# Pooling the key and value maps after their projection instead of pooling their input

## The chip, the cores and the metric

The program runs on one core of a Trainium2 chip. Its metric is the device time of one execution in microseconds (us); lower is better. A core has five engines that run side by side, each with its own queue in order: TensorE (PE, matrix products), VectorE (DVE), ScalarE (ACT, activations), GpSimd (POOL) and SyncE (SP, which issues DMAs). They wait for one another through semaphores. All data is fp32.

## The reference, cut to what matters

The input is 8 images of 256 channels at 32x32. Two layers follow; the change is in the first, a convolutional attention:

```python
q = einsum('bchw,oc->bohw', x, q_w)               # x is group-normalised
kv = einsum('bchw,oc->bohw', x, kv_w)
k_map, v_map = kv[:, :C], kv[:, C:]
def pooled(t):
    for i, r in enumerate([1, 2, 3, 6]):          # 32x32, 16x16, 11x11, 5x5
        p = einsum('bchw,ph,qw->bcpq', t, Mh, Mw) # mean over windows
        p = p + depthwise3x3(p, dconv_w[i], dconv_b[i])
    return concat of all p                        # 1024 + 256 + 121 + 25 = 1426 tokens
k = layernorm(pooled(k_map)); v = layernorm(pooled(v_map))
attn = softmax(q_g @ k^T * SCALE); out = attn @ v # 8 heads of 32 channels
```

Pooling works on positions and the projection on channels, so the two can be exchanged: a map projected from pooled x equals the pooled projection of x. After some mixing by head and a projection, layer 1 does self-attention over the 1024 tokens of each image, and a mixture of 8 experts (three dense steps each) over all tokens.

## The kernel before, in words

Channels lie on partitions, in two blocks of 128. An image of x is `xi`, [128, 2, 1024]. Keys and values are four maps of 128 channels and 1426 columns: m = 2 and 3 are values, 0 and 1 keys.

**Order of work.** The class `Flow` writes the program out ahead of time. It keeps an estimated clock for every engine, prices each instruction (`cost`) and emits them in one order per engine (`note`). Pieces of work are generators ("threads") with a rank. Before each piece they say what they wait for: `pe(...)`, `ve(...)`, `act(...)`, `pool(...)` or a condition (`until`). `step` runs those that are ready by the estimate and that fit: PE work fits when it ends before the score tile comes free, and within a credit of PE time per step (4.0 us for ranks under 5, 2.0 us for ranks from 5 on, which are layer 1). `finish` runs threads until a condition holds, ready or not. Every instruction of a flow has the line of the helper (669) in the profile, so the tile names tell the rows apart.

**The backbone** is a loop of 384 steps: 8 images x 2 channel blocks x 2 halves of the queries x 12 chunks of 128 keys (the last has 18). A step is the scores of one chunk for four heads (`sc`, one PSUM tile of four banks, one buffer), the exponential on ACT into `pt`, and the products with the values (`pv`) of the step before. Every second step POOL issues a DMA that adds one `pt` to the other (`pt<-pt`), and DVE adds such pairs up for the softmax sum. An image is 48 steps. The steps of image b + 1 can't begin before its keys are there: the loop calls `finish` on `key_parts`.

**Threads beside it**, by rank: keys and values to tokens (2; `keys_and_values`, `value_tokens`, `key_tokens`), preparation of the next image (4; `prepare`, with `pool_levels`, `maps`, `queries`), layer 1 and the set-up of its weights (5, 6), and the depthwise convolution (7; `convolve`).

- `prepare(b)` loads and normalises `xi`. `pool_levels(xi, xl)` makes the three pooled levels of x in `xl`, [128, 2, 402]: 16x16 and 11x11 on POOL (ten operations per block), 5x5 on DVE (5 reductions along rows, 5 along columns, one scaling).
- `maps` projects the four maps. Each has slices of 512, 512 and 402 columns (`KEY_SLICES`), the last from `xl`. A slice is two products of 128x128 weights with the slice, in PSUM (`sm` or `sx`). ACT copies it to `p` (`pmap`, one buffer) and, with bias and the middle tap (plus 1 for the identity), into the sum `acc` (three buffers).
- `taps` adds the other eight taps of a level on DVE, in place: acc = p * w + acc. `convolve` runs the four levels of one map after the other. `read` counts maps whose full-size level is convolved (then `p` may be overwritten there), `done` those that are finished, `freed` buffers given back.
- `queries` projects q from `xi` and stores it in DRAM.
- For image 0 `first_maps`, `first_keys` and `first_taps` do the same with more help from PE.

While the score loop runs, products with 128 weight columns are issued as four of 32 columns (`f.columns`, `narrow`). [...]one product of a 512- or 402-column slice with one of the two channel blocks leaves 8 records in the trace.

After the last step the remaining layer-1 work and the experts follow; expert passes run ahead of the gate while layer 1 ends, their results parked in DRAM. The program also holds a general version of everything, for inputs whose softmax sums go out of range; it is compiled, and skipped at the end by a branch.

Of the kernel before, what the change touches and what calls it, by code (L numbers as in the profile page):

```python
# [16 lines left out]
P = 128  # L17
# [638 lines left out]
class Flow:  # L656
# [162 lines left out]
    def keys(self, a):  # L819

        name = self.key(a)
        cut = self.cut.get(name)
        if cut is None:
            return [name]
        return [f"{name}/{i}" for i in range(len(cut) - 1) if cut[i] < a.offset + a.free_size() and a.offset < cut[i + 1]]
# [69 lines left out]
def attention(tc, kit, f, outer, ended, nb, consts, x, t1, t2, hn, bounds, vecs, q_t, kv_t, proj_t, gqk_t, wqk, wqkv, vecs1, w1_d, w1c, gate_d, wrc, vecs2, bnvec):  # L895
# [6 lines left out]
    with ExitStack() as ctx:  # L902
# [57 lines left out]
        )  # L960
        hi, lo = bounds
# [105 lines left out]
        todo, done, read, freed, key_parts, normalised = [], [], [4], [0], [0], [0]  # L1067
# [20 lines left out]
        def maps(xp):  # L1088

            for m in (2, 3, 0, 1):  # L1090
                c = m % 2
                yield until(lambda: read[0] >= len(todo) and len(todo) < 3 + 2 * freed[0])
                p = pmap
                acc = T(work, [P, NK], "acc", bufs=3)
                for s0, w in KEY_SLICES:
                    if s0 >= HW:
                        yield until(lambda: len(done) >= len(todo))
                    src = source(xp, s0, w)
                    yield pe(src, tag="sm")
                    ps = small()  # L1100
                    for k in range(2):
                        f.pe.matmul(
                            ps[:, :w],
                            lhsT=kvw[:, k, m * P : (m + 1) * P],
                            rhs=src[:, k, :],
                            start=k == 0,
                            stop=k == 1,
                        )
                    f.act.activation(p[:, s0 : s0 + w], ps[:, :w], AF.Copy)
                    for s, n in enumerate(SIDES):  # L1110
                        a, z = max(OFFS[s], s0), min(OFFS[s] + n * n, s0 + w)
                        if a < z:
                            f.act.activation(
                                acc[:, a:z],
                                ps[:, a - s0 : z - s0],
                                AF.Identity,
                                bias=db(c, s),
                                scale=mid[:, c * 4 + s : c * 4 + s + 1],
                            )
                todo.append((c, p, acc))  # L1120
# [7 lines left out]
        pmap = T(work, [P, NK], "p")  # L1128
        f.split(pmap, 512, HW)
# [14 lines left out]
        def first_maps(xp):  # L1144


            for m in range(4):
                if m < 2:
                    p = T(work, [P, 4, 512], "pt", bufs=6).rearrange("p j q -> p (j q)")
                    acc = T(l1, [P, NK], "v") if m else T(work, [P, NK], "kn", bufs=3)  # L1150
                else:
                    p = T(work, [P, NK], "acc", bufs=3) if m == 3 else pmap
                    acc = T(work, [P, NK], "acc", bufs=3)
                for t in (p, acc):
                    if t is not pmap:
                        f.split(t, 512, HW)
                first[m] = p, acc
            for m, s0 in [(m, s0) for g in (0, 2) for s0 in (0, 512) for m in (g, g + 1)] + [(m, HW) for m in range(4)]:
                if s0 == HW:
                    yield until(lambda: pooled)  # L1160
                w = min(512, NK - s0)
                c = m % 2
                p, acc = first[m]
                src = source(xp, s0, w)
                yield pe(src, tag="sm")
                ps = small()
                for k in range(2):
                    f.pe.matmul(
                        ps[:, :w],
                        lhsT=kvw[:, k, m * P : (m + 1) * P],  # L1170
                        rhs=src[:, k, :],
                        start=k == 0,
                        stop=k == 1,
                    )
                f.act.activation(p[:, s0 : s0 + w], ps[:, :w], AF.Copy)
                for s, n in enumerate(SIDES):
                    a, z = max(OFFS[s], s0), min(OFFS[s] + n * n, s0 + w)
                    if a < z and (m >= 2 or s):
                        f.act.activation(
                            acc[:, a:z],  # L1180
                            ps[:, a - s0 : z - s0],
                            AF.Identity,
                            bias=db(c, s),
                            scale=mid[:, c * 4 + s : c * 4 + s + 1],
                        )
                if (m, s0) == (3, 512):
                    large.append("maps")
                    f.spawn(first_keys(0), 1)
                    f.spawn(first_keys(1), 5)
            whole.append("maps")  # L1190
# [24 lines left out]
        def taps(c, s, p, acc):  # L1215
            n, o = SIDES[s], OFFS[s]
            pin = p[:, o : o + n * n].rearrange("p (h w) -> p h w", h=n)
            pout = acc[:, o : o + n * n].rearrange("p (h w) -> p h w", h=n)
            for tap in range(9):
                if tap == 4:  # L1220
                    continue
                dy, dx, y0, y1, x0, x1 = windows(tap, n)
                o_ap = pout[:, y0:y1, x0:x1]
                yield ve(pin[:, y0 + dy : y1 + dy, x0 + dx : x1 + dx], o_ap)
                f.ve.scalar_tensor_tensor(
                    o_ap, pin[:, y0 + dy : y1 + dy, x0 + dx : x1 + dx], dw(c, s, tap), o_ap, ALU.mult, ALU.add
                )

        def first_taps():
            for m in (2, 3):  # L1230
                yield until(lambda: "maps" in large)
                yield from taps(m - 2, 0, *first[m])
                large.append(("values", m))
            yield until(lambda: whole)
# [4 lines left out]
            done.extend(first[m][1] for m in (2, 3, 0, 1))  # L1239

        def convolve():

            for m in range(4, 4 * nb):
                yield until(lambda: len(todo) > m)
                c, p, acc = todo[m]
                for s in range(4):
                    yield from taps(c, s, p, acc)
                    read[0] += s == 0
# [51 lines left out]
        def pool_levels(xi, xl):  # L1300
# [6 lines left out]

            for k in range(2):
                one, l2, l3 = img[:, k], level(1)[:, k], level(2)[:, k]

                yield pool(xi)
# [3 lines left out]
                f.pool.tensor_tensor(l2, t2[:, 0::2, :], t2[:, 1::2, :], ALU.add)  # L1315
                yield pool(t2)
                f.pool.tensor_scalar(l2, l2, 0.25, 1.0, ALU.mult, ALU.mult)

                yield pool(xi)
                t3 = T(work, [P, 32, 11], "pool")  # L1320
                f.pool.tensor_tensor(t3, one[:, :, 0::3], one[:, :, 1::3], ALU.add)
                yield pool(t3)
                f.pool.tensor_tensor(t3[:, :, 0:10], t3[:, :, 0:10], one[:, :, 2::3], ALU.add)
                yield pool(t3)
                f.pool.tensor_tensor(t3[:, :, 1:11], t3[:, :, 1:11], one[:, :, 2::3], ALU.add)
                yield pool(t3)
                f.pool.tensor_tensor(l3, t3[:, 0::3, :], t3[:, 1::3, :], ALU.add)
                f.pool.tensor_tensor(l3[:, 0:10, :], l3[:, 0:10, :], t3[:, 2::3, :], ALU.add)
                yield pool(t3)
                f.pool.tensor_tensor(l3[:, 1:11, :], l3[:, 1:11, :], t3[:, 2::3, :], ALU.add)  # L1330
                flat = xl[:, k, OFFS[2] - HW : OFFS[3] - HW]
                f.pool.tensor_tensor(flat, flat, con[:, K_S11 : K_S11 + 121], ALU.mult)

            t5 = T(work, [P, 2, 32, 5], "pool")
# [4 lines left out]
            yield ve(t5, xl)  # L1339
            l5 = level(3)  # L1340
            for i, (a, e) in enumerate(ends):
                f.ve.tensor_reduce(
                    l5[:, :, i, :], t5[:, :, a:e, :].rearrange("p k h w -> p k w h"), AX.X, ALU.add
                )
            flat = xl[:, :, OFFS[3] - HW :]
            f.ve.tensor_tensor(flat, flat, con[:, None, K_S5 : K_S5 + 25].to_broadcast([P, 2, 25]), ALU.mult)
            pooled.append(True)

        def prepare(b):
# [35 lines left out]
            xl = T(work, [P, 2, NK - HW], "xl")  # L1385
            if b == 0:
                f.spawn(pool_levels(xi, xl), 2)
            else:
                yield from pool_levels(xi, xl)
            xp = xi, xl  # L1390
            if b == 0:
                todo.extend([None] * 4)
                f.spawn(queries(b, xi), 3)
                yield from first_maps(xp)
            else:
                yield from maps(xp)
# [64 lines left out]
        def keys_and_values(b):  # L1461
# [10 lines left out]
            if b == 0:  # L1472
                yield until(lambda: len(vts[b]) == 3)
                freed[0] += 1
# [1075 lines left out]
```

## Time and profile before

| | before |
|---|---|
| runs, us | 3309.33, 3313.4, 3316.51; median 3313.4 |
| profiled execution, us | 3310.0 (span 3308.1) |
| mean granted TensorE clock | 0.979 |
| matmul records | 23038 |

The span is the time from the first to the last instruction of the profiled execution; 1.9 us lie around it. Busy time of an engine is the time in which at least one of its instructions runs. PE instructions overlap, so a group's busy time is smaller than count times mean, and the distance of two starts is the better price of a group. A wait is put down to the instruction that released it.

### The profile page before, as it was taken

Reading aid. Unit: us, or ns where it says so; the run is one execution under the profiler, and the core shown is the slowest. Engines: PE = TensorE matmul, PEld = TensorE weight load, DVE = VectorE, ACT = ScalarE, POOL = GpSimd, SP = SyncE. Lnnn points to the kernel's source line nnn. Section 1 sums busy time; section 2 is a strip of 40 time slices with the busy share of each in tenths; the row PEclk is TensorE's granted clock in tenths of the full one; section 3 lists DMA queues with packets and bytes.
Section 4 is the critical chain, followed back from the end, with each engine's and each line's share of the span. In section 5 each row is a group of like instructions: output and inputs, shape, how many; then the busy total and the mean of one; then the engine's idle time right before and its main releaser. Section 6 shows DMA issues by size and latency. Waiting matters only on the chain. (4 is left out here: it accounts for less than half of the span.)

```text
span 3308.1 us, 57168 instructions
## 1 busy us (share of the span) xinstructions
PE 3098.8 (94%) x23038; PEld 1790.7 (54%) x23038; DVE 2455.2 (74%) x4068; ACT 1733.4 (52%) x2330; POOL 1217.1 (37%) x1315
## 2 busy tenths in 40 slices
PE   8687899999999999999899889999999999999997
PEld 4322234334334334334334236767888888888886
DVE  5687688797886887987875455447888787777776
ACT  4476675675676576666666543343333344444442
POOL 2211411412213213213112112007656567777775
PEclk9798999999999999999999999999999999999999
DMA  2357655745646756655556557125434310000000
GB/s 75 84 127 165 131 100 145 147 93 143 142 103 143 147 132 131 132 133 114 125 127 143 122 119 246 60 86 178 153 134 153 139 65 20 20 25 27 20 14 21
DMA packets 110754, 362.70 MB, mean 110 GB/s; under 512 B 13504, under 2 KB 38856, under 8 KB 87248
## 3 DMA queue, kind: packets, MB, share of 16 engines
q0 software_dynamic: 28608, 179.85, 28.2%
q1 hardware_dynamic: 78512, 177.13, 15.5%
q8 instruction: 184, 3.01, 0.4%
q10 hardware_dynamic: 3360, 1.97, 0.2%
q14 instruction: 90, 0.74, 0.1%
HBM read 112.45 MB, written 81.31 MB: 59 GB/s over the span
## 5 line engine op out<-in xcount | busy, mean ns | idle before, releaser
L669 ACT ACTIVATE pt<-sc 128x2048 f32<-128x2048 f32 (+1 forms) x384 | 720.5, 1876 | 298.5 <-PE sc L669 246.5
L669 DVE SCALAR_TENSOR_TENSOR acc<-p,vec,acc 128x225 f32<-128x225 f32 (+7 forms) x928 | 532.7, 580 | 31.3 <-ACT acc L669 6.5
L669 PE MATMUL sc<-q,kn 32*128 32x512 f32 (+1 forms) x3072 | 448.1, 653 | 108.0 <-ACT pt L669 105.8
L669 DVE TENSOR_TENSOR pt<-pt,pt 128x1024 f32<-128x1024 f32 x320 | 384.4, 1244 | 144.3 <-DMA pt<-pt 133.1
L669 POOL DMA_DIRECT2D pt<-pt x192 | 171.4, 894 | 769.3 <-ACT pt L669 592.9
L669 PE MATMUL pv<-pt,vt 128*32 128x512 f32 (+1 forms) x3072 | 420.2, 620 | 0.0
L669 ACT ACTIVATE p1c<-bank 128x256 f32<-128x256 f32 x230 | 87.9, 382 | 565.9 <-PE bank L669 554.3
L669 ACT ACTIVATE h<-h,bnvec 128x512 f32<-128x512 f32 x460 | 348.0, 805 | 63.8 <-DVE h L669 54.7
L669 POOL TENSOR_TENSOR rstd<-rstd,mhalf 128x4 f32<-128x4 f32 (+2 forms) x88 | 108.8, 1237 | 697.7 <-DVE rstd L669 586.3
L669 DVE TENSOR_TENSOR h<-p1c,bank 128x512 f32<-128x512 f32 x230 | 156.7, 681 | 211.6 <-PE bank L669 211.0
L669 PEld LDWEIGHTS sc<-q,kn 32*128 32x128 f32 (+1 forms) x3072 | 116.8, 179 | 320.2 <-ACT pt L669 217.8
L669 POOL TENSOR_TENSOR tm<-h,tm 128x256 f32<-128x256 f32 x210 | 241.8, 1151 | 16.5
L669 DVE TENSOR_TENSOR h<-u,bank 128x256 f32<-128x256 f32 x460 | 234.3, 550 | 7.9
L669 PEld LDWEIGHTS pv<-pt,vt 128*32 128x32 f32 (+1 forms) x3072 | 60.9, 108 | 304.2 <-issue 295.1
L669 POOL TENSOR_TENSOR tm<-h 128x512 f32<-128x512 f32 x105 | 137.9, 1313 | 195.2 <-ACT h L669 194.1
L669 DVE TENSOR_TENSOR h<-h,gate 128x1024 f32<-128x1024 f32 x128 | 203.2, 1588 | 0.5 <-ACT h L669 0.5
L669 PE MATMUL bank<-h,w2e 128*128 128x256 f32 (+1 forms) x604 | 193.3, 448 | 2.8 <-DVE h L669 1.9
L669 PE MATMUL sm<-p,v 128*32 128x256 f32 (+1 forms) x2416 | 192.3, 379 | 0.7 <-ACT p L669 0.7
L669 PE MATMUL y<-t,s3e 128*128 128x256 f32 x768 | 187.0, 379 | 2.2 <-POOL t L669 2.1
L669 PE MATMUL bank<-t,s1e 128*128 128x256 f32 x750 | 183.8, 381 | 3.5 <-DVE h L669 3.5
L669 POOL TENSOR_TENSOR t<-h,t 128x256 f32<-128x256 f32 x216 | 172.9, 800 | 17.0
L669 POOL TENSOR_TENSOR t<-h 128x512 f32<-128x512 f32 x108 | 140.1, 1298 | 105.4 <-DVE h L669 80.0
(315 smaller groups left out, 5448.6 us busy)
## 6 DMA issues: line engine op xcount, KB each, us to landing
pt<-pt POOLq DMA_DIRECT2D x160, 1024.0 KB, 7.5
h<-h SPq DMA_DIRECT2D x118, 512.0 KB, 3.3
xi<-in_x_dram SPq DMA_DIRECT2D x16, 512.0 KB, 6.7
t<-t SPq DMA_DIRECT2D x8, 1024.0 KB, 5.6
res<-t SPq DMA_DIRECT2D x32, 256.0 KB, 4.7
t<-res SPq DMA_DIRECT2D x32, 256.0 KB, 4.6
hn<-res SPq DMA_DIRECT2D x32, 256.0 KB, 4.2
hn<-hn SPq DMA_DIRECT2D x16, 512.0 KB, 4.4
```

The costliest lines, as they stand in the source:

```text
L669: ins = fn(*args, **kwargs)
```

## The change

Image 0 keeps its way: its x is pooled and its maps are projected in three slices. From image 1 on:

- `maps` takes x alone. It projects the maps in two pairs (values, then keys), each map in two slices of 512 columns, copies them to a pair of maps (`pmap`, now [128, 2, 1426]) and starts `acc` for the full-size level. When all earlier maps are finished, it calls `pool_levels` on the pair, which makes the pooled levels from the projected maps, and starts `acc` of each pooled level from `pmap` in SBUF with three ACT operations per map.
- `pool_levels` does the 11x11 sums of both blocks in one operation, drops the scaling of the 16x16 level (the 0.25 goes into that level's weights, once, at the start), and has a buffer of its own for the 5x5 rows.
- `convolve` works in pairs: the full-size level of both maps, then the pooled levels of each, when `levels` says that they are there.
- `acc` has four buffers. `xl` no longer has a buffer; image 0 uses one of the value tokens' buffers.
- `keys` tells the parts of the paired `pmap` apart for the order of work.
- The program reserves 4096 bytes per partition for the descriptors of POOL's DMAs, where the default is 16384.

```diff
+        quarter = vec[:, V_DW : V_DW + 72].rearrange("p (c s t) -> p c s t", c=2, s=4)[:, :, 1, :]
+        f.ve.tensor_scalar(quarter, quarter, 0.25, None, ALU.mult)
+        f.ve.tensor_scalar(mid[:, 1::4], mid[:, 1::4], 0.25, None, ALU.mult)
...
-        def maps(xp):
-
-            for m in (2, 3, 0, 1):
-                c = m % 2
-                yield until(lambda: read[0] >= len(todo) and len(todo) < 3 + 2 * freed[0])
-                p = pmap
-                acc = T(work, [P, NK], "acc", bufs=3)
-                for s0, w in KEY_SLICES:
-                    if s0 >= HW:
-                        yield until(lambda: len(done) >= len(todo))
-                    src = source(xp, s0, w)
...
+        def maps(xi):
+
+            for part in range(2):
+                n = len(todo)
+                accs = []
+                for c in range(2):
+                    m = 2 - 2 * part + c
+                    yield until(lambda: read[0] >= n + c and n + c < 6 + 2 * freed[0])
+                    acc = T(work, [P, NK], "acc", bufs=4)
+                    accs.append(acc)
+                    for s0 in range(0, HW, 512):
+                        src = xi[:, :, s0 : s0 + 512]
+                        yield pe(src, tag="sm")
+                        ps = small()
+                        for k in range(2):
+                            f.pe.matmul(
...
+                        f.act.activation(pmap[:, c, s0 : s0 + 512], ps, AF.Copy)
+                        f.act.activation(
+                            acc[:, s0 : s0 + 512],
+                            ps,
+                            AF.Identity,
...
+                    todo.append((c, pmap[:, c, :], acc))
+                yield until(lambda: len(done) >= n)
+                yield from pool_levels(pmap[:, :, :HW], pmap[:, :, HW:])
+                for c in range(2):
+                    for s in range(1, 4):
+                        o, w = OFFS[s], SIDES[s] ** 2
+                        yield act(pmap[:, c, o : o + w])
+                        f.act.activation(
+                            accs[c][:, o : o + w],
+                            pmap[:, c, o : o + w],
+                            AF.Identity,
+                            bias=db(c, s),
+                            scale=mid[:, c * 4 + s : c * 4 + s + 1],
                         )
+                    levels[0] += 1
...
-        pmap = T(work, [P, NK], "p")
-        f.split(pmap, 512, HW)
+        pmap = T(work, [P, 2, NK], "p")
+        f.split(pmap, 512, HW, NK, NK + 512, NK + HW)
...
-            for m in range(4, 4 * nb):
-                yield until(lambda: len(todo) > m)
-                c, p, acc = todo[m]
-                for s in range(4):
+            for n in range(4, 4 * nb):
+                yield until(lambda: len(todo) > n)
+                c, p, acc = todo[n]
+                if n % 2 == 0:
+                    yield from taps(c, 0, p, acc)
+                    read[0] += 1
+                    yield until(lambda: len(todo) > n + 1)
+                    yield from taps(*todo[n + 1][:1], 0, *todo[n + 1][1:])
+                    read[0] += 1
+                yield until(lambda: levels[0] > n)
+                for s in range(1, 4):
                     yield from taps(c, s, p, acc)
-                    read[0] += s == 0
                 done.append(acc)
...
-                f.pool.tensor_tensor(l2, t2[:, 0::2, :], t2[:, 1::2, :], ALU.add)
-                yield pool(t2)
-                f.pool.tensor_scalar(l2, l2, 0.25, 1.0, ALU.mult, ALU.mult)
...
+                f.pool.tensor_tensor(l2[:, k], t2[:, 0::2, :], t2[:, 1::2, :], ALU.add)
+            t3 = T(work, [P, 2, 32, 11], "pool")
...
+            yield pool(t3)
+            f.pool.tensor_tensor(l3, t3[:, :, 0::3, :], t3[:, :, 1::3, :], ALU.add)
...
-            t5 = T(work, [P, 2, 32, 5], "pool")
+            t5 = T(work, [P, 2, 32, 5], "pool5")
...
-            xl = T(work, [P, 2, NK - HW], "xl")
             if b == 0:
+                xl = T(work, [P, 2, NK - HW], "vt", bufs=6)
                 f.spawn(pool_levels(xi, xl), 2)
-            else:
-                yield from pool_levels(xi, xl)
-            xp = xi, xl
...
-                yield from maps(xp)
+                yield from maps(xi)
...
-            if b == 0:
-                yield until(lambda: len(vts[b]) == 3)
-                freed[0] += 1
+            yield until(lambda: len(vts[b]) == 3)
             freed[0] += 1
...
-    nc = _bacc.Bacc("TRN2", target_bir_lowering=False, num_devices=1)
+    nc = _bacc.Bacc("TRN2", target_bir_lowering=False, num_devices=1, dynamic_dma_scratch_size=4096)
```

## The prediction

> **What bounds the kernel now.** I read the page first, then the busy time by stage, then the timeline of TensorE inside one image, then the waits, then the groups of the pooling. The profiled execution took 3310.0 us (span 3308.1 and 1.9 around it), 3.4 under the median of the runs, 3313.4.
>
> ```profile
> PE 3098.8 (94%) x23038; PEld 1790.7 (54%) x23038; DVE 2455.2 (74%) x4068; ACT 1733.4 (52%) x2330; POOL 1217.1 (37%) x1315
> 80.00:1953.00 1873.00, 1722.38 (x17026) 667.30 (x17026) 1441.22 (x2566) 1203.54 (x1439) 444.57 (x527) 0.97 0.60 128
> 1953.00:3308.00 1355.00, 1311.35 (x5838) 1091.51 (x5836) 968.88 (x1404) 498.67 (x825) 752.99 (x753) 0.99 0.24 86
> ```
>
> The two stages (columns: length, then PE, PEld, DVE, ACT, POOL busy, clock, DMA share, GB/s) part at the last score step. From 80 to 1953 the 384 score steps of layer 0 run, with everything else as filler; after 1953 the rest of layer 1 and the experts. PE is busy 92% of the first and 97% of the second; no other engine passes 77% in the first.
>
> In the PE timeline (start, length, idle before in brackets) one step looks like this:
>
> ```profile
> 861.57 1.14 PE L669 MATMUL sc<-q,kn 32*128 32x512 f32 x8
> 862.64 1.06 PE L669 MATMUL pv<-pt,vt 128*32 128x512 f32 x8
> 864.71 1.14 PE L669 MATMUL sc<-q,kn 32*128 32x512 f32 x8 [1.00 <-ACT pt L669]
> ...
> 870.06 1.06 PE L669 MATMUL pv<-pt,vt 128*32 128x512 f32 x8
> 870.95 1.54 PE L669 MATMUL sx<-xl,kvw 128*32 128x402 f32 x16
> 872.41 1.14 PE L669 MATMUL sc<-q,kn 32*128 32x512 f32 x8
> ```
>
> The first step has no filler: scores, values, then 1.00 us of waiting for the exponential of the scores, because the score tile has one buffer. It takes 3.14 us. The next one shown has filler (`xl`, the work that the change removes) and no wait. So a step lasts as long as its PE work, but never under about 3.15 us. The waits say the same; of 85 us in 350:1850, 72 are this one:
>
> ```profile
> PE sc L669 <- ACT pt L669: 72.4, 76, 4.7
> PE sm L669 <- DVE res L669: 7.0, 3, 4.4
> ```
>
> [...]the 992-element depthwise tap took 1.15 us at best and 1.27 us in the mean. [...]Here the 512-element pooling add took 1.29 us in the mean, a VectorE add of that size 0.69. [...]The trace shows some 131 packets per transfer, about 8 for each of 16 DMA engines, one transfer per two steps; I count nothing for it[...].
>
> **The change, part by part.**
>
> *Removed from PE.* For seven images, four maps each, the 402-column slice goes: 28 slices. By the timeline one slice is 16 records, 870.95 to 872.41: 1.46 us. 28 x 1.46 = -40.9 us. It is PE time in a stage where PE is busy 92%.
>
> *Moved.* I laid the PE instructions of both programs, in the order in which they issue, over the score steps, and priced each by timeline rows: scores 1.07, values 1.00, a 512-column product 0.90 (859.30 less 857.59 is two products), 402 columns 0.73, 256 columns 0.43, a transpose 0.145. For the old program that gives 1692 us in the steps; the trace has 1722. For the new one it gives 1627, 65.4 less, though only 40.9 are gone. The other 24.5 are layer-1 work that now stands behind the last step: 16 products y,t and 28 products p,v (44 x 0.43 = 18.9), 4 of t,gw (3.6), 8 transposes (1.2) and small ones (0.8). Layer 1 has a fixed credit of PE time per step and fills what the exponential covers; shorter steps give it less. Its gaps between images also move to where other filler has run out.
>
> *Steps at their floor.* Under 3.15 us of PE work stand 105 steps of the old order and 123 of the new. In the old trace steps of that kind, the first twelve left out, took 3.46 us in the mean, while steps over 3.6 us took their PE work within some 2%. Filled up to 3.46, the old order loses 119.8 us and the new one 141.9: +22.1. So the score stage goes by -65.4 + 22.1 = -43.3.
>
> *After the last step.* The 24.5 us land in a stretch where PE is busy (232.6 of 247 us in 1953:2200), so +24.5. One more pass of the experts runs ahead of the gate and one more of its second products is done the plain way, 4 x 0.90 instead of 7 x 0.43: +0.6. Sum so far: -43.3 + 25.1 = -18.2.
>
> *Added to VectorE.*
>
> ```profile
> L669 DVE TENSOR_REDUCE pool<-xi 128x64 f32<-128x448 f32 x24 | 13.6, 610 | 13.3 <-POOL xl L669 13.3
> L669 DVE TENSOR_REDUCE xl<-pool 128x10 f32<-128x70 f32 x24 | 5.6, 275 | 0.2
> ```
>
> One pooling to 5x5 is 5 x 0.62 + 5 x 0.28 + 0.21 = 4.7 us. It was done once per image on x and is done twice on pairs of maps: +4.7 us per image, 33 in all. The 13.3 us in which VectorE waited for GpSimd's buffer go, as this pooling has its own buffer. VectorE idles 271 of 1421 us in 324:1745, 45 per image.
>
> *Added to GpSimd.* Its pooling groups (adds and scalings) sum to 98 us for six images, 16.4 each. The 0.25 scaling goes (1.3), leaving 15.1, and the 11x11 sums are joined for two maps (four operations, 0.84, 0.61, 0.61 and 0.45 us for one map, now once per pair at double width; I take 1.6 of 5.0 as saved): about 13.5 per pair, 27 per image, +10.6 per image, 74 us in all. GpSimd is 25% busy there, so its own time is covered. What is queued behind it are the adding DMAs of the probabilities (one per two steps) and the powers of the normalisations. VectorE waits for both. [...]The taps that meet now lose 0.12 of 1.27 us. I take 4 per image.
>
> *ACT.* Four 402-column copies of 0.51 us go per image. The pooled levels' scaled copies now read SBUF: 12 per image, 0.56, 0.46 and 0.38 us from PSUM. [...]They wait for the VectorE pooling, and exponentials stand behind them.
>
> *No cost.* Folding 0.25 into the taps is two short operations ahead of the first statistics (0.3 us). The queries and token work are the same instructions. Four convolution buffers replace three, and the gate now lets all four maps of the next image through; projections start at steps 1 to 5 of an image instead of 5 to 10 in most, which costs nothing by itself.
>
> *Charge.* VectorE gets 4.7 + 4 us per image and the image is some 6 us shorter, so its idle time falls from 45 to about 30. ACT waited 34 us for taps in 325:1745, with exponentials behind. For more of that I charge +5 in all (between 0 and the rival's price). Forecast: 3310.0 - 18.2 + 5 = 3296.8 in a profiled execution; beside the median 3313.4 - 13.2 = 3300.
>
> **Rivals.**
>
> *The whole PE saving shows.* If the short steps lose no more than before, 40.9 are gained: 3272. The order speaks against it (18 more short steps); for it, that PE bounds nearly all the rest.
>
> *Nothing is left.* If short steps cost 3.7 instead of 3.46 (+3 more) and VectorE and ACT take 15, the sum is zero: 3307 to 3320. The 21 steps of 2.8 to 3.2 us of PE work already took 3.9 in the mean, which speaks for it.
>
> *VectorE's chain becomes the bound: slower.* The second pair of maps now goes through projection, GpSimd pooling (13.5), VectorE pooling (4.7), scaled copies and 48 small taps before its tokens, where before the pooled x lay ready. The convolution has the lowest rank. In the new order the first key-token transposes of images 4 to 7 stand at steps 47, 47, 47 and 45 of the image before, against the 48th step that needs them (42, 47 or 45 to 47 before). If the chain is late on the chip, the next image's scores wait.[...] 18.2/7 = 2.6 us per image eat the gain; 5 to 8 per image give +17 to +38, so 3330 to 3351. Against it: 30 us of VectorE idle time per image.
>
> That the change does not do what it says is out: in the new order the 402-column products stand in the first image alone.
>
> **How the numbers follow.** Likeliest, a gain of 7 to 30 us (3283 to 3306): 0.46. Over 30: 0.08. Within 0.2% (6.6 us; what a measurement of this kernel can tell from no change): 0.19. VectorE's chain: 0.27, of which about 0.1 lies over 3332. The range 3278 to 3332 leaves out that and half of the second case. The likeliest case has its own range, 3283 to 3306.
>
> **What would show it.** In the new profile: no `xl` products after the first image; PE busy time down by about 40; the last score step at about 1910 instead of 1953, and 25 us more between it and the end; more waits of PE for the exponential (72 to about 90 in the same stretch). VectorE up by 33 to 60 us. The prediction is wrong if waits of PE for key tokens, or of ACT for pooled maps with the exponential behind, pass some 2.6 us per image, or if the layer-1 rest behind the last step meets idle PE time.

## The result, and the profile after

| | before | after |
|---|---|---|
| median, us (4 runs each) | 3314.87 | 3354.48 |
| lowest and highest | 3309.33, 3316.51 | 3352.79, 3359.1 |
| profiled execution, us (span) | 3310.0 (3308.1) | 3355.3 (3353.5) |
| first score to last score step, profiled | 1873.0 | 1907.7 |
| last score step to the end, profiled | 1354.8 | 1366.8 |

The changed kernel takes 1.0125 times as long, 95% interval [1.0107, 1.0142]. The forecast was 3300, and 3354 also lies above its range (3278 to 3332). The score stage was to become 43 us shorter and became 35 us longer: 78 us are to be found there. The part after it was to become 25 us longer and became 12 us longer.

The busy times of the changed kernel:

```profile
PE 3087.4 (92%) x22416; PEld 1784.9 (53%) x22416; DVE 2522.0 (75%) x4146; ACT 1725.0 (51%) x2301; POOL 1330.7 (40%) x1359
```

By stage (length, then PE, PEld, DVE, ACT, POOL busy, clock, DMA share, GB/s), parted at its last score step:

```profile
79.00:1987.00 1908.00, 1689.90 (x16282) 643.50 (x16286) 1499.26 (x2616) 1190.66 (x1400) 565.58 (x581) 0.96 0.59 126
1987.00:3353.00 1366.00, 1333.02 (x5962) 1109.77 (x5954) 976.68 (x1428) 502.91 (x835) 747.90 (x749) 0.99 0.25 89
```

The removed products are gone: TensorE is busy 32 us less in the first stage. But it idles 218 us there instead of 151, and GpSimd is busy 566 us instead of 445. TensorE's waits, in the stretch in which they were read before:

```profile
PE sc L669 <- ACT pt L669: 93.2, 81, 5.9
PE sm L669 <- DMA t<-t: 11.9, 2, 10.0
PE sx L669 <- DMA t<-t: 6.2, 1, 6.2
```

The wait for the exponential grew from 72.4 to 93.2, and two waits of layer 1 for a transfer are new. Over the whole stage the first grew from 106 to 146 us. The waits for key tokens, on which the slower rival rests, did not grow: those for `kt` fell from 12.8 to 6.9 us, and the scores' for the finished keys (`kn`) rose from 0.8 to 5.1. So the rival's total (3330 to 3351) is close, but its place is not.

What did grow are the taps of the convolution and GpSimd's sums. VectorE and GpSimd groups of 325:1745, first before, then after:

```profile
L669 DVE SCALAR_TENSOR_TENSOR acc<-p,vec,acc 128x992 f32<-128x992 f32 x96 | 121.6, 1266 | 2.2
L669 POOL TENSOR_TENSOR pool<-pool,xi 128x320 f32<-128x320 f32 x24 | 26.0, 1084 | 1.4
```

```profile
L669 DVE SCALAR_TENSOR_TENSOR acc<-p,vec,acc 128x992 f32<-128x992 f32 x96 | 138.1, 1438 | 4.5 <-POOL p L669 2.4
L669 DVE TENSOR_REDUCE pool<-p 128x64 f32<-128x448 f32 x48 | 27.4, 611 | 13.5 <-POOL p L669 13.5
L669 POOL TENSOR_TENSOR pool<-pool,p 128x320 f32<-128x320 f32 x48 | 78.0, 1624 | 3.1
```

The same tap takes 0.17 us longer and the same sum 0.54 us longer. The new reductions cost what was said (611 ns), but VectorE's wait for GpSimd before them, which was to go (13.3 us before), is still there (13.5). All of GpSimd's sums in that stretch add up to 209 us for 12 pairs, 17.4 each, where 13.5 were forecast.

The mean of the tap hides two kinds. In that stretch of the trace after, 32 of the 96 taps overlap one of GpSimd's sums and take 1.82 us in the mean; the other 64 take 1.23 to 1.25. VectorE's adds of two `pt` behave alike: 26 beside a sum take 1.72, the other 208 take 1.22. Its reductions don't: 23 beside a sum take 0.613, the other 25 take 0.610. Before, none of the 96 taps overlaps a sum of x.

One place shows how this reaches TensorE. A pair of maps of a later image is being pooled. The timeline (start, length, idle before in brackets) of GpSimd, VectorE, ScalarE and TensorE:

```profile
858.33 3.72 POOL L669 TENSOR_TENSOR pool<-pool,p 128x320 f32<-128x320 f32 x2
...
869.83 0.65 POOL L669 TENSOR_TENSOR p<-p,con 128x242 f32<-128x242 f32 x1
870.43 0.88 POOL L669 DMA_DIRECT2D t<-xr  x1
871.03 1.18 POOL L669 DMA_DIRECT2D pt<-pt  x1
```

```profile
861.11 3.77 DVE L669 TENSOR_TENSOR pt<-pt,pt 128x1024 f32<-128x1024 f32 x2
864.80 1.93 DVE L669 SCALAR_TENSOR_TENSOR acc<-p,vec,acc 128x961 f32<-128x961 f32 x1
```

```profile
863.44 0.69 ACT L669 ACTIVATE xr<-sm,mtb 128x512 f32<-128x512 f32 x1 [2.56 <-PE sm L669]
...
870.52 0.49 ACT L669 ACTIVATE acc<-p,vec,mid 128x121 f32<-128x121 f32 x1 [3.64 <-POOL p L669]
870.91 1.86 ACT L669 ACTIVATE pt<-sc 128x2048 f32<-128x2048 f32 x1
```

```profile
863.31 1.14 PE L669 MATMUL sc<-q,kn 32*128 32x512 f32 x8
...
872.82 1.14 PE L669 MATMUL sc<-q,kn 32*128 32x512 f32 x8 [3.15 <-ACT pt L669]
...
889.21 1.12 PE L669 MATMUL sm<-con,t 128*128 128x128 f32 x4 [10.05 <-DMA t<-t]
890.12 1.06 PE L669 MATMUL sx<-con,t 128*128 128x128 f32 x4
891.11 2.09 PE L669 MATMUL sc<-q,kn 32*128 32x512 f32 x8
```

Two things happen. **The overlap:** while the sums run, two adds of VectorE take 3.77 us (2.35 at 881.93, when none runs) and a tap of 961 elements 1.93 (1.21 in the mean in e13 below). **The queue:** `xr` is stored at 864.1, but GpSimd's DMA of it is issued at 870.43, behind the sums. ScalarE's scaled copy waits 3.64 us for the sums, with an exponential queued behind it, and TensorE waits 3.15 us for that exponential, then 10.05 us for `t`. (Scaled copies wait for the sums only twice in the whole stage, 4.0 us in all.) After that gap the scores take 2.09 us instead of 1.14, and the granted clock is 0.50 from 881.3 to 898.2: the halving came some 2 us after TensorE's last product, which ended at 879.2.

### The profile page after: what moved, and what is told of

It reads as the page before. It is cut to its first block, busy times and chain, and to the rows that moved or that the text cites. A ratio compares the mean times of both kernels' runs of the same rounds, so it can differ in the third digit from the quotient of the medians.

```text
span 3353.5 us, 55997 instructions
## 1 busy us (share of the span) xinstructions
PE 3087.4 (92%) x22416; PEld 1784.9 (53%) x22416; DVE 2522.0 (75%) x4146; ACT 1725.0 (51%) x2301; POOL 1330.7 (40%) x1359
## 5 line engine op out<-in xcount | busy, mean ns | idle before, releaser
L669 DVE SCALAR_TENSOR_TENSOR acc<-p,vec,acc 128x961 f32<-128x961 f32 (+3 forms) x960 | 581.6, 613 | 75.6 <-ACT acc L669 39.5
L669 PE MATMUL sc<-q,kn 32*128 32x512 f32 (+1 forms) x3072 | 455.8, 664 | 152.4 <-ACT pt L669 146.4
L669 DVE TENSOR_TENSOR pt<-pt,pt 128x1024 f32<-128x1024 f32 x320 | 391.8, 1268 | 93.4 <-DMA pt<-pt 91.3
L669 DVE TENSOR_TENSOR u<-h,bank 128x512 f32<-128x512 f32 x229 | 157.4, 687 | 24.8 <-PE bank L669 0.5
```

What stands on the lines that cost most here:

```text
L669: ins = fn(*args, **kwargs)
```

## The experiments

Four theories stood at the start: GpSimd's sums are what costs, through the longer operations of VectorE that they overlap (1a; a tap above took 1.82 us beside a sum, 1.23 to 1.25 elsewhere) or through what waits behind them in GpSimd's queue (1b); VectorE's second 5x5 pooling (2); the smaller descriptor rings, that is 4096 bytes for the descriptors of POOL's DMAs in place of 16384 (3); the pairing and its order of work (4). The results at a glance (ratio to the kernel before, from its runs on the same chip; stage and tap of 992 elements from the profiled execution):

| run | us | ratio, 95% interval | score stage, us | tap, us |
|---|---|---|---|---|
| before | | | 1873.0 | 1.266 |
| after | 3354.5 | 1.0125 [1.0107, 1.0142] | 1907.7 | 1.438 |
| e1, no GpSimd sums | 3259.1 | 0.9848 [0.9829, 0.9866] | 1812.7 | 1.265 |
| e2, no 5x5 | 3331.8 | 1.0064 [1.0044, 1.0083] | 1871.8 | 1.440 |
| e3, neither | 3242.2 | 0.9797 [0.9778, 0.9817] | 1794.8 | 1.273 |
| e4, before, no 402-column products | 3277.0 | 0.9904 [0.9881, 0.9926] | 1832.5 | 1.249 |
| e5, powers for sums | 3304.8 | 0.9986 [0.9977, 0.9995] | 1874.7 | 1.257 |
| e6, sums on VectorE | 3298.6 | 0.9954 [0.9938, 0.9969] | 1869.5 | 1.250 |
| e7, sums at a higher planned price | 3365.3 | 1.0168 [1.0141, 1.0195] | 1931.3 | 1.455 |
| e8, before, x pooled twice | 3423.2 | 1.0334 [1.0300, 1.0368] | 1988.2 | 1.250 |
| e9, before, small rings | 3303.1 | 0.9978 [0.9967, 0.9989] | 1881.5 | 1.254 |
| e10, 11x11 on VectorE | 3328.5 | 1.0055 [1.0038, 1.0072] | 1883.2 | 1.314 |
| e11, 16x16 on VectorE | 3349.8 | 1.0123 [1.0106, 1.0139] | 1919.2 | 1.395 |
| e12, before, sums on VectorE | 3335.4 | 1.0070 [1.0053, 1.0087] | 1870.0 | 1.272 |
| e13, same order, queue held | 3304.3 | 0.9982 [0.9974, 0.9990] | 1859.5 | 1.248 |
| e14, same order, not held | 3292.6 | 0.9937 [0.9917, 0.9957] | 1846.9 | 1.248 |

### Which part costs: e1, e2, e3

From image 1 on, e1 leaves out the 16x16 and 11x11 sums, e2 the 5x5 pooling, e3 both; the rest runs on whatever stands in the buffers.

```diff
+            if not pooled:              # e1: image 0 alone
                 for k in range(2):
                     one = img[:, k]
...
                     f.pool.tensor_tensor(t2, one[:, :, 0::2], one[:, :, 1::2], ALU.add)
```

> The changed kernel without the 16x16 and 11x11 sums on GpSimd from image 1 on; those levels then hold what image 0 left in the pair of maps, so that part of the computation is left out. Theory 1 (GpSimd's queue: [...]the adding DMAs and stores queued behind them come late): most of the 40 us come back, and the PE saving shows; 3285 to 3305. Theory 2 (VectorE's own extra work, 33 us of 5x5 pooling): 3335 to 3350. Theory 3 (smaller descriptor rings) and theory 4 (pairing, gates and order of work): 3340 to 3355.

> The changed kernel without the 5x5 pooling on VectorE from image 1 on; that level then holds what image 0 left, so that part is left out. Theory 1: VectorE gets 66 us back, part of which is slack, 3330 to 3350. Theory 2: 3290 to 3310. Theories 3 and 4: 3345 to 3355.

> The changed kernel with neither pooling from image 1 on (all pooled levels left as image 0 left them, so that part is left out): paired maps, four convolution buffers, small descriptor rings and the shorter projection alone. Theories 1 and 2: about 3285, as the PE work of the steps, filled up to 3.15 us each, and of the rest falls by 29 us. Theory 3 or 4: 3330 to 3355, slower than the kernel before although the pooling costs nothing.

Without GpSimd's sums the kernel is 95 us faster than the changed one and the tap is back at 1.265 us; without the 5x5 it is only 23 us faster, and the tap stays at 1.44. Theory 2 is no more than a part, and the loss sits with GpSimd's sums. With neither, the kernel is 68 us faster than before, so nothing points to the pairing or the small rings (4 and 3). e1 and e3 came out 26 and 43 us under the lowest time that any theory had for them (3285): these runs let the program order its work anew, which the last pair below shows to matter.

### The removed products alone: e4

The kernel before, without the 402-column products (from image 1 on); ScalarE reads the pooled x in their place, so the pooled levels aren't projected.

```diff
-                    yield pe(src, tag="sm")
-                    ps = small()
...
+                    if s0 < HW:
+                        yield pe(src, tag="sm")
+                        ps = small()
...
+                    else:
+                        yield act(src)
+                        ps = src[:, c, :]
```

> The kernel before without the 402-column products from image 1 on; ACT reads the pooled x itself, so the projection of the pooled levels is left out. All else stays, pooling included. What the PE saving is worth alone: by the steps filled up to 3.15 us and the work behind them -34, so about 3281 under every theory that I hold; 3310 if the saving is worth nothing because other engines set the steps.

3277.0, 33 us under the 3309.9 of the kernel before in those runs; 3281 was expected. The score stage is 40.5 us shorter, the end 9 us longer. So of the 40.9 us of removed products some four fifths can be had, though this program too is ordered anew. The first term of the forecast holds; the error is to be looked for in what was added.

### Overlap or queue, a first look: e5

In place of the sums, seven powers of 8 columns and a few products of 8 columns per pair, with inputs from the pair. The sums are left out, and GpSimd is held about as long: 256 us in all for these, 245 us for the changed kernel's sums.

```diff
+                for u in range(7):
+                    yield pool(z)
+                    f.pool.tensor_tensor(z, z, kit.mhalf[:, 0:1].to_broadcast([P, 8]), ALU.pow)
```

> The changed kernel with the pooling sums on GpSimd replaced, from image 1 on, by seven powers of 128x8 (2.0 to 2.3 us each) and six tiny products, some 17.5 us per pair in the same place: the queue is held as long as by the sums, but hardly any data is read. The 16x16 and 11x11 levels are left out. Theory 1a[...]: the 992-element tap falls from 1.44 to about 1.27 us and the time to 3275 to 3300. Theory 1b (queue: DMAs that stand behind the sums): 3335 to 3355, with the tap short again.

3304.8, 50 us less than the changed kernel, with the tap at 1.257. Holding GpSimd's queue as long, without reading much of SBUF, costs far less than the sums do; the time is a little over what was expected under theory 1a. But this program too was ordered anew.

### The sums on VectorE: e6, e10, e11

These compute everything, with the sums of images 1 to 7 on VectorE: all of them (e6), the 11x11 alone (e10), the 16x16 alone (e11).

```diff
+            pl, e = (ve, f.ve) if pooled else (pool, f.pool)
...
-                yield pool(t2)
-                f.pool.tensor_tensor(l2[:, k], t2[:, 0::2, :], t2[:, 1::2, :], ALU.add)
+                yield pl(t2)
+                e.tensor_tensor(l2[:, k], t2[:, 0::2, :], t2[:, 1::2, :], ALU.add)
```

> The changed kernel with the 16x16 and 11x11 sums on VectorE from image 1 on: [...]some 13.6 us more VectorE work per image. By the second run 9.4 us per image of VectorE work cost 22 us, so this costs about 32 over the first run: 3285 to 3305. If VectorE's load is what binds (theory 2): over 3340.

> The changed kernel with the 11x11 sums on VectorE from image 1 on and the 16x16 sums still on GpSimd (4 of 14 operations, some 5 of 17.5 us per pair). [...]the 992-element tap at 1.28 to 1.33 us and, between the changed kernel (3354) and all sums on VectorE (3299), nearer to the latter: 3300 to 3322.[...]

> The changed kernel with the 16x16 sums on VectorE and the 11x11 sums still on GpSimd (10 of 14 operations, some 12.4 us per pair). The larger dose: tap at 1.36 to 1.42 us, 3325 to 3350, slower than the run with the 11x11 sums moved.[...]

The tap grows with the sums left on GpSimd, from none to the 16x16, the 11x11 and all: 1.250, 1.314, 1.395, 1.438 us. The time follows less well: 3299, 3328, 3350, 3354 us. e10 is over its forecast (3300 to 3322), e11 can't be told from the changed kernel by its ratio, and its stage is longer (1919.2 against 1907.7) though the taps are shorter. These orders of work differ too. VectorE gets more to do in e6 (busy 1232 us of 325:1745, against 1187 after) and the kernel is faster all the same. e6 computes everything and beats both kernels: 0.9954 of the kernel before, a gain of about 15 us (the medians of all runs, 3309.6 and 3298.6, are 11 apart).

### A plan with dearer sums: e7

```diff
+            if self.columns and self.key(out).split("_")[0] in ("pool", "p"):
+                return 0.15 + 0.0036 * n
```

> The changed kernel, planned with a price of 0.15 us + 3.6 ns per element for the pooling sums instead of 2.3 ns, so that the planner expects what the trace showed (17.5 us per pair instead of 12.3). Same work. If the loss is that instructions are placed for a chain that ends earlier than it does: 3315 to 3335.[...]

3365.3: no better than the changed kernel, and over the 3315 to 3335 of a loss by placement. That the planner underrates the sums isn't the cause.

### Controls on the kernel before: e8, e9, e12

e8 runs x's pooling twice, e9 takes the small descriptor rings alone, e12 moves x's sums to VectorE as in e6. All three compute everything.

```diff
                 yield from pool_levels(xi, xl)
+                yield from pool_levels(xi, xl)           # e8
...
+    nc = _bacc.Bacc("TRN2", target_bir_lowering=False, num_devices=1, dynamic_dma_scratch_size=4096)   # e9
```

> The kernel before, with its pooling of x done twice in a row per image from image 1 on (the second overwrites the first with the same values): +16.7 us of GpSimd and +4.7 us of VectorE work per image, without any PE saving. The steps filled up to 3.15 us say +26. If a second pooling costs what it costs in the changed kernel (some 95 us for GpSimd's sums in two runs, against none): +40 to +60, 3350 to 3370. If it only hurts beside the taps of its own maps: +20 to +30, 3330 to 3340.

> The kernel before with 4096 instead of 16384 bytes per partition for the descriptors of GpSimd's DMAs, nothing else. Theory 3[...]: slower, 3320 to 3350. All other theories: no difference, 3303 to 3317.

> The kernel before with the 16x16 and 11x11 sums of x on VectorE from image 1 on (6.8 us per image, once), nothing else. In the kernel before these sums do not stand beside the big taps of the same image. [...]+10 to +20 for the VectorE work, 3318 to 3330. If GpSimd's sums cost there too (the run without any pooling was 35 us faster than the one without the 402-column products): 3285 to 3305.

e8 missed what every theory expected: 3423. Its taps stay at 1.250, so longer taps aren't why. In the kernel before, all maps of an image stand behind the pooling of x. Its waits of TensorE:

```profile
PE sc L669 <- ACT pt L669: 119.7, 119, 4.5
PE sm L669 <- ACT kt L669: 20.4, 19, 12.0
PE sx L669 <- ACT kt L669: 11.7, 15, 4.4
```

Key tokens are waited for 32 us, against 13 before, as the slower rival had it, but in another kernel; that is 19 of the 71 us by which TensorE's idle time in the stage grew, and the rest was not followed. As a test of the sums' price the run was ill chosen. e9: the small rings cost nothing. e12: in the kernel before, GpSimd's sums don't stretch the taps (1.266 with them, 1.272 without). Moving them makes it 0.7% slower (3335, over the forecast of 3318 to 3330), but not in the score stage (1870.0): the end is 33 us longer, with another order of work. In the kernel before the sums run while x is prepared; in the changed kernel they run beside the taps of their own maps.

### The same order of every queue: e13, e14

Each edit so far made the program order its work anew, so part of each difference is a difference of plans. These two keep the changed kernel's order on every engine and queue. Each sum is replaced in its place: in e14 by a product of one column, in e13 by that and a power of one column, which holds GpSimd about as long without reading much. The 16x16 and 11x11 sums are left out. The traces agree: all else on every engine and queue is the same list in the same order, but for one fill of a constant at the start. The waits are nearly the same; a stand-in reads one column, so the first one on a pair's second map waits for half of that map, where a sum waits for all of it. The lowest range that e13 was given, 3265 to 3300, is for the overlap as the larger part.

```diff
+            def stand(out, a, b, op):             # o, i0: one column of out and of an input
...
+                ins = nc.gpsimd.tensor_tensor(o, i0, i0, ALU.mult)
...
+                ins = nc.gpsimd.tensor_tensor(z, z, kit.mhalf[:, 0:1], ALU.pow)   # e13 alone
+                f.note("POOL", "tensor_tensor", ins, (out, a, b, op), {})
```

> The changed kernel with every instruction of TensorE, VectorE, ScalarE and the DMA queues in the order of the changed kernel, and GpSimd's queue too, but each of its 14 sums per pair (images 1 to 7) replaced in its place by a product of one column with the same waits and a power of one column, about 1.2 us together as against 1.2 to 1.3 us for a sum in the mean. Left out: the 16x16 and 11x11 sums. GpSimd's queue is held about as long[...]. [...](71 of the 93 us over the plan without sums, as the powers of an earlier run suggested, though in another order), about 3283 (3265 to 3300), taps of 992 elements back at 1.27 us. If holding the queue is what costs, 3330 to 3355 with the taps at 1.27. If the earlier figure came from the other order alone, anything between.

> The same with the power left out too, so that each of the 14 sums is a product of one column with the same waits (about 0.4 us): the same order of every queue[...]. Left out: the 16x16 and 11x11 sums. Both theories: 3255 to 3275, with GpSimd's poolings the whole of the loss over the forecast's 3300 and more. The difference to the kernel with powers is the price of holding the queue alone, 10 to 25 us[...], 60 to 90 by the queue theory. If this one stays above 3300, the loss is in the order, which no earlier run has kept the same.

The groups of 325:1745 of e13:

```profile
L1346 POOL TENSOR_TENSOR zz<-zz,mhalf 128x1 f32<-128x1 f32 x168 | 138.6, 825 | 0.0
L669 DVE SCALAR_TENSOR_TENSOR acc<-p,vec,acc 128x992 f32<-128x992 f32 x96 | 119.8, 1248 | 2.2
L1338 POOL TENSOR_TENSOR pool<-p 128x1 f32<-128x1 f32 x96 | 71.2, 749 | 25.1 <-ACT p L669 25.1
```

Records of such short operations overlap. Taken together, powers and products cover 199 us there, 16.6 per pair; the sums cover 208, or 17.3, and the products alone, in e14, 88, or 7.3. From the start of a pair's first sum to the end of its last pass 26 us in the mean after, 20 in e13 and 17 in e14. The stage lasts 1846.9 us with the products alone (e14), 1859.5 with the queue held (e13) and 1907.7 with the sums (after). **Holding the queue costs 12.6 us, the sums in place of the stand-ins 48.2.** The runs say the same: by their ratios, 0.9937, 0.9982 and 1.0125, it is 15 us, give or take 7, and 47, give or take 6. The first figure is rough: before and e9, which have one order of work, differ by 8 us in this stage. It prices the 9 us per pair by which e13 holds GpSimd longer than e14, so the whole hold may cost more. The second is the overlap with VectorE's operations in the main (the tap takes 1.438 us after, 1.248 in e13 and e14), with what e13 lacks of the sums' time.

TensorE's waits for `t` in 325:1745, in e13 and then in e14:

```profile
PE sm L669 <- DMA t<-t: 11.1, 2, 10.1
PE sx L669 <- DMA t<-t: 7.8, 1, 7.8
```

```profile
PE sm L669 <- DMA t<-t: 4.4, 1, 4.4
PE sx L669 <- DMA t<-t: 2.7, 1, 2.7
```

These 11.8 us are nearly all of the queue's price, and they come from three waits; after, they are no longer than in e13 (18.1). At e14's place of the stall shown above, ScalarE and TensorE answer so:

```profile
837.72 0.69 ACT L669 ACTIVATE xr<-sm,mtb 128x512 f32<-128x512 f32 x1 [2.56 <-PE sm L669]
838.78 1.88 ACT L669 ACTIVATE pt<-sc 128x2048 f32<-128x2048 f32 x1 [0.38 <-PE sc L669]
840.56 0.97 ACT L669 ACTIVATE acc<-p,vec,mid 128x256 f32<-128x256 f32 x2
```

```profile
837.58 1.14 PE L669 MATMUL sc<-q,kn 32*128 32x512 f32 x8
...
844.51 1.14 PE L669 MATMUL sc<-q,kn 32*128 32x512 f32 x8 [0.57 <-ACT pt L669]
...
854.12 1.11 PE L669 MATMUL sm<-con,t 128*128 128x128 f32 x4 [4.42 <-DMA t<-t]
855.02 1.06 PE L669 MATMUL sx<-con,t 128*128 128x128 f32 x4
856.01 2.09 PE L669 MATMUL sc<-q,kn 32*128 32x512 f32 x8
```

From 837.58 to 856.01 are 18.4 us; the same instructions took 27.8 after (863.31 to 891.11). The wait for the exponential shrinks from 3.15 to 0.57, that for `t` from 10.05 to 4.42. In e13 the longest wait for `t` is still 10.1: that one belongs to the queue.

Both missed: e13 took 3304.3, just over its 3265 to 3300, and e14 3292.6, not 3255 to 3275. Holding the order fixed, the sums cost 62 us (3354.5 less 3292.6), not e1's 95. The other 33 us lie between e14 and e1, whose stage stands 34 us under e14's. e1 has another order and no stand-ins; no run parts the two.

## Why the prediction was wrong, by its own steps

**The steps that held.** *Removed from PE:* -40.9 was forecast, and e4's stage is 40.5 us shorter; with the change TensorE's busy time in the stage fell by 32. *Steps at their floor:* with the order of the changed kernel and no sums, steps with less than 3.15 us of TensorE work last 3.43 us in the mean (3.46 forecast). *After the last step:* TensorE's busy time there grew by 22.0 (24.5 were said to move), but its idle time fell from 43.7 to 33.0, so the end came only 12 us later: part of that work met idle time, which the prediction had named as a sign against it. *Nothing for the rings:* e9. *ACT:* the pooled levels' copies take 0.589, 0.478 and 0.399 us in the mean from SBUF after and 0.562, 0.458 and 0.384 from PSUM before, 14 to 27 ns longer; little hangs on it.

**Two signs that came near for another reason.** In 350:1850 the waits for the exponential came to 93 us (about 90 forecast, from shorter steps), but in e14, with that order and no sums, they are 74. VectorE's busy time rose by 67 us (33 to 60 forecast), but in e14, with both 5x5 poolings, it is 4 us below the kernel before. Both rises came with the sums.

**The sum without the added engines.** It was -18.2. e14, which has the new order and VectorE's reductions, but products of one column for GpSimd's sums (7.3 us per pair), has a span 16.1 us under the kernel before, and 20.8 by its ratio, interval 14 to 27. The forecast is right through two errors: the stage gained 26.1 where 43.3 were forecast, and the end lost 10.6 where 25.1 were. Of the stage's part, steps over 3.6 us were taken to last their work "within some 2%"; they did before (5.38 us for 5.30 priced), but in the new order they last 5.38 us for 5.19, 242 times. The clock accounts for this: the 227 of them at full clock last 5.20 us for 5.17, and the 15 that meet a stretch with a granted clock of 0.50 run 42 us over their prices (before, 9 such steps, 25 us). Such stretches make up 133 us of e14's stage and 102 of the stage before; why there are more stays open.

**The step that failed** is "Added to GpSimd", with the charge that follows from it. Two sentences are wrong.

- "GpSimd is 25% busy there, so its own time is covered." The DMAs and the powers queued behind the sums were named, then priced at nothing. Held by stand-ins that leave the taps at 1.248 us (e13), the queue costs 12.6 us or more, by way of the transfers of `t`, which the list of what is queued did not have.
- "I take 4 per image", the author's estimate, with +5 in all for its effect on the end. This is the larger term: 48.2 us of the stage. VectorE's instructions add up to 2682 us after, 2611 in e13 and 2612 in e14: the sums in place of the stand-ins cost VectorE 70 us, 10 per image. It is lost in meetings: the taps take 1.82 us beside a sum and 1.25 elsewhere. VectorE's reductions, with one input, take the same in all three (611, 608 and 607 ns). GpSimd's own sums pay as well (1.624 us against 1.084), which made them 17.4 us per pair instead of 13.5.

The 4 rested on "the taps that meet now lose 0.12 of 1.27 us". The trace before had no such meeting to read: its taps overlap no sum of x, and the 85 of 96 beside no GpSimd arithmetic at all take 1.25 us in the mean. (The other 11 take 1.42, beside other work of GpSimd.) In the changed kernel a pair is pooled just when its full-size taps run, and a tap that meets a sum loses 0.57 us. Nor is the growth of GpSimd's time, 10.6 us per image, a measure of the loss: what can lie beside VectorE's operations is all 27 us of sums per image (35 as measured). The 10.6 was also read from sums of 98 us in 350:1850, which is not six whole images; in 325:1745 they are 102.5. (A 512-column product is 0.90 in the prediction and 0.855 by its own two starts. The orders before and after have nearly the same number of these, so little follows.)

The 78 us of the stage are thus 17.2 (long steps at half clock, in the main), 12.6 (longer hold of the queue) and 48.2 (the sums themselves, their overlap with VectorE's operations in the main).

**The idle time.** The argument that VectorE had 45 us of idle time per image, so that 9 more would fit, was the wrong measure. While a pair is pooled VectorE runs without a gap (848.83 to 866.7 in the timeline), then waits 3 us for the sums; what it delays there, the adds that free the exponentials' buffers, is due within a step or two. In the stage, exponentials wait for the adding DMAs and VectorE's adds 73 us after, 53 in e13, 51 in e14. All of ScalarE's waits for VectorE add up to 132 us after, 85 in e13 and 86 in e14, and all of TensorE's for ScalarE to 173, 133 and 137. So most of the 48 us passes from VectorE to ScalarE, whose queue is in order, and from there to TensorE. TensorE's idle time accounts for 41 of it (218 against 177 in e13) and slower products for the rest. VectorE itself waits 43 us for GpSimd after and 17 in e13, so the lateness of the sums has a share in this, which no run parts from VectorE's longer operations.

**The rivals.** "The whole PE saving shows" and "nothing is left" stayed too low for the same reason. "VectorE's chain becomes the bound" had the sign and nearly the time; its place, late key tokens at the start of an image, is refuted by the 12.0 us of such waits (`kt` and `kn`), 1.7 per image, against 13.6 before. ScalarE's waits for pooled maps are 13.5 us, 1.9 per image. So neither of these signs passed the 2.6 per image at which the prediction would call itself wrong: the loss came by a way that it did not watch.

## What to carry to other kernels

Work that moves to GpSimd is not free because GpSimd is idle: price it once on the queue (which DMAs and which engines' copies stand behind it) and once on VectorE, by what it runs in that very stretch, not by the mean over the stage. Ask which operations will lie beside the moved sums, and price a meeting from a trace in which they do meet; a mean over a kernel in which they don't says nothing. Here the sums were better on VectorE itself, although it was the busier engine. And when a part is taken out to find its price, keep the order of everything else: removing these sums gave 95 us with a new plan, and 62 with the old one and short stand-ins in their place.

## What was not expected of the hardware

- Where sums and VectorE's operations overlapped, both took longer: VectorE 70 us in all, and GpSimd's sum of 320 elements went from 1.08 to 1.62 us.
- Products of one column leave the taps short (1.248 us in e14), but free the queue only in part: fourteen of them hold GpSimd 7.3 us per pair, where fourteen sums hold it 17.3. Short operations of GpSimd take longer themselves beside VectorE's taps and adds: in 325:1745 after, a power of four columns (`rstd`) takes 1.76 us in the mean beside one (11 of them) and 1.03 elsewhere (24). The taps don't notice the powers of e13 (1.248 us).
